# Local transformer on Trainium2: inverse key norms spread over the partitions by two transfers in place of a matmul

## The chip, the cores and the metric

The kernel runs on one core of one Trainium2 chip. The core has a matrix engine (PE, with its weight loads listed apart as PEld), a vector engine (DVE), a scalar engine (ACT), a general engine (POOL), and a queue (SP) from which this kernel issues all its DMA transfers. The engines run side by side and wait for one another by semaphores. The metric is the device time of one execution in microseconds (us), lower is better. It is given as the median of several runs. A separate execution was taken with the hardware profiler; every duration of single instructions comes from that one.

## The reference

The program is a chain of twelve stages on activations of 8 sequences of 256 tokens and 128 features, all in fp32: mixtures of experts, several kinds of attention, a state-space layer, and twice the same small local transformer of six layers. Only this local transformer is touched. Its attention, cut to what matters (`d` = 64, 16 heads, `w` = 32):

```python
def l2norm(t):
    return t / jnp.maximum(jnp.linalg.norm(t, axis=-1, keepdims=True), 1e-12)

def attn_layer(x, Wqkv, qs, ksc, Wo):
    q, k, v = jnp.split(x @ Wqkv, 3, -1)
    q, k, v = (sh(q), sh(k), sh(v))              # (batch, head, token, 64)
    q = l2norm(q) * qs
    k = l2norm(k) * ksc
    q = q * cos * scale + rotate_half(q) * sin * scale
    inv = 1.0 / scale
    k = k * cos * inv + rotate_half(k) * sin * inv
    out = local_attention(q, k, v)               # windows of 32 queries, 64 keys, softmax
    return out.transpose(0, 2, 1, 3).reshape(b, n, INNER) @ Wo
```

Each layer is `x = attn_layer(shift_tokens(x), ...) + x` and then `x = ffn_layer(shift_tokens(x), ...) + x`, where the second is a layer norm, a gated GELU network and a residual. What the change touches is the norm of the keys: every key of every head is divided by its length over the 64 features of the head.

## The kernel before, in words

**Groups and quads.** The 8 sequences are worked on in 4 groups of 2 sequences, so a tile has 128 partitions (features) and T = 512 columns (tokens). The 16 heads are taken four at a time: a *quad* is one group, one layer and four heads. Four heads of 64 features are 256 features, held as two tiles side by side (`j` = 0, 1), each with two heads over its 128 partitions. Six layers, four groups and four quads of each make 96 quads in a pass of the local transformer, 192 in the program.

**The pipeline.** `ffn2` runs three quads at a time, each in another phase. In one turn of its loop `q0` is projected and normalised, `q1` (the quad before) is scored, put through softmax and weighed with the values, and `q2` (the one before that) is turned back and handed on. The calls of a turn come in a fixed order: scores of `q1`, projection of `q0`, exponential of `q1`, `quad_back` of `q2`, `quad_norms` of `q0`, `quad_done` of `q2`, `quad_values` of `q0`, `quad_turn` of `q1`, `quad_scale` of `q0`, `quad_weigh` of `q1`. A wrapper (`_Ordered`) makes PE, DVE, ACT and POOL each keep the order in which their instructions are written, so a waiting instruction holds up everything behind it on its engine. Only the SP queue is ordered by the framework's scheduler.

**Pieces.** When the fourth quad of a group has been handed on, the group's output projection (`local_tail`: matmuls `wo_acc`, the residual `x`, the shifted copy `l_xs`, the layer norm `ln_c`, `ln_sq`, `ln_r`) is cut into pieces and put between the calls of one turn, and the gated network (`local_geglu`: matmuls `ge` and `w_acc`, GELU `l_gl`, product `l_ag`) into those of the next turn. So four turns make a cycle. If c is the number of the quad `q0` in its group, the turns c = 1 carry the tail, c = 2 the gated network, and c = 3 and c = 0 carry no pieces.

**The norms.** In `quad_project` PE makes `pp` (the projection), ACT squares it into `l_sq`, DVE multiplies it by the sine table (`l_y`) and by the cosine table (`l_yk` for the keys, `l_yq` for the queries), and four transfers exchange neighbouring partitions of the sine product into `l_yr` (the rotation's other half). In `quad_norms` the matrix `hsum` adds the squares over a head's partitions: four matmuls into one bank, and ACT makes the inverse square root, `l_rn`. Of each 32 rows of `l_rn` two hold something, one for each head; rows 0 to 63 belong to the queries and 64 to 127 to the keys. POOL adds the rotation's half to the keys (`l_yk`).

In `quad_scale`, 16 small matmuls with `hpick` bring the queries' inverse norms to where the softmax needs them (`tp`, which the profile calls bank, into `l_rq`), and two matmuls with `hrow` spread the keys' inverse norms from their two rows over each head's 64 partitions (`rb`). DVE then clamps `rb`, multiplies it into the keys and writes `l_kp`, and after that it adds the rotation's half to the queries (`l_yq`). `quad_scores` of the next turn reads both `l_kp` and `l_yq` in 128 small matmuls `sc`.

**Memory banks.** Most matmul results rotate through three double banks (`two`: `sc`, `pp`, `pp`, `ct`, `vp`, `et`, `rb`, `cx`, `cx`, and `ge`), so each of these waits until what was written three places before has been read. `l_sq` has two buffers.

Of the kernel before, what the change touches and what calls it, by code (L numbers as in the profile page):

```python
# [24 lines left out]
ALU = mybir.AluOpType  # L25
# [3 lines left out]
P = 128  # L29
B, S, D = 8, 256, 128  # L30
NB = 2
T = NB * S
# [6 lines left out]
WIN = 32  # L39
# [13 lines left out]
def _constants():  # L53

    f = np.float32
    p = np.arange(P)
    c = {}
    c["ident"] = np.eye(P, dtype=f)
    c["mean"] = np.full((P, P), 1.0 / P, f)
    c["ones"] = np.ones((P, P), f)  # L60
    c["iota"] = np.tile(np.arange(E, dtype=f), (P, 1))
    c["krow"] = (p % 32 == DH).astype(f)[:, None]
    c["eps"] = np.tile(
        np.array([1e-5, 2e-5, 2.0**-64, 0.5 * SH * math.log(2.0)], f), (P, 1)
    )
    blk = (p[:, None] // 64 == p[None, :] // 64).astype(f)
    c["blkm"] = blk / f(64)

    z = np.zeros((P, 32), f)
    z[:64, 0] = 1.0  # L70
    z[64:, 1] = 1.0
    c["hsum"] = z
    z = np.zeros((P, P), f)
    z[0::32, :64] = 1.0
    z[1::32, 64:] = 1.0
    c["hrow"] = z
    z = np.zeros((P, 4), f)
    for n, r in enumerate((0, 32, 1, 33)):
        z[r, n] = 1.0
    c["hpick"] = z  # L80

    r = np.zeros((P, P), f)
    for m in range(P):
        if m % 2 == 0:
            r[m + 1, m] = -1.0
        else:
            r[m - 1, m] = 1.0
    c["rot2"] = r

    sel = np.zeros((P, 4, P), f)  # L90
    for g in range(4):
        for j in range(4):
            for d in range(DH):
                sel[DH * (4 * g + j) + d, g, 32 * j + d] = 1.0
    c["sel"] = sel.reshape(P, -1)


    lev = [np.eye(P, dtype=f)]
    for i in range(7):
        n = 2**i  # L100
        q = p // n
        lev.append(((q[:, None] % 2 == 0) & (q[None, :] == q[:, None] + 1)).astype(f))
    c["lev"] = np.concatenate(lev, 1)

    c["cq"] = np.where(p[None, :] > p[:, None], f(NEG), f(0))
    c["ck"] = np.where(p[:, None] > p[None, :], f(NEG), f(0))
    one9 = np.zeros((P, 32), f)
    one9[:, DH] = 1.0
    c["one9"] = one9
    m = np.zeros((P, 2, 64), f)  # L110
    i, key = p % 32, np.arange(64)
    ok = (key[None, :] >= i[:, None]) & (key[None, :] <= i[:, None] + WIN)
    m[:, 0, :] = np.where(ok & ((p[:, None] >= 32) | (key[None, :] >= 32)), f(0), f(LNEG))
    m[:, 1, :] = np.where(ok, f(0), f(LNEG))
    c["lmask"] = m.reshape(P, -1)

    half = np.arange(0, 64, 2, dtype=f)
    inv_freq = f(1.0) / f(10000.0) ** (half / f(64))
    t = np.arange(S, dtype=f)
    fr = t[:, None] * inv_freq[None, :]  # L120
    fr = np.concatenate([fr, fr], -1).T
    base = (half + f(0.4 * 64)) / f(1.4 * 64)
    sc = base[None, :] ** ((t - f(S // 2)) / f(WIN // 2))[:, None]
    sc = np.concatenate([sc, sc], -1).T
    two = lambda a: np.concatenate([_partners(a.T).T] * 2, 0).astype(f)

    sgn = np.where(p[:64, None] < 32, f(1), f(-1))
    c["qcos"] = two(np.cos(fr) * sc * f(8.0))
    c["qsin"] = two(np.sin(fr) * sc * f(8.0) * sgn)
    c["kcos"] = two(np.cos(fr) * (f(1.0) / sc))  # L130
    c["ksin"] = two(np.sin(fr) * (f(1.0) / sc) * sgn)

    i = np.arange(DH // 2, dtype=f)
    th = np.power(f(10000.0), f(-2.0) * (i - f(1.0)) / f(DH))
    ang = t[:, None] * th[None, :]
    per = lambda a: np.tile(np.repeat(a.T, 2, axis=0), (NH, 1)).astype(f)
    c["rcos"] = per(np.cos(ang))
    c["rsin"] = per(np.sin(ang))

    groups = {  # L140
        "c1": ("ident", "mean", "ones", "iota", "krow", "eps"),
        "cs0": ("cq", "ck"),
        "cs1": ("lev", "blkm"),
        "cs2": ("hsum", "hrow", "hpick", "lmask", "qcos", "qsin", "kcos", "ksin"),
        "cs3": ("rot2", "sel", "ck", "one9", "rcos", "rsin"),
    }
    return {n: {k: c[k].astype(f) for k in ks} for n, ks in groups.items()}
# [10 lines left out]
def _partners(w):  # L158

    w = np.asarray(w)  # L160
    return w.reshape(w.shape[:-1] + (2, 32)).swapaxes(-1, -2).reshape(w.shape)
# [16 lines left out]
def _layout(inp):  # L178
# [72 lines left out]
    }  # L251
    a, at = {}, {}
    packs = {"pv": pv, "w0": w0, "wt": wt, "w1": w1, "w2": w2, "w3": w3, **_constants()}
    for name, parts in packs.items():
        a[name], at[name] = _pack(parts)
# [49 lines left out]
class _Net:  # L305
# [976 lines left out]
    def two(self, name):  # L1282
        return self.psp2.tile([P, 2, T], F32, tag="mm2", name=name)
# [48 lines left out]

    def quad_norms(self, q):

        nc = self.nc
        sp = self.ps()
        for s, (n, j) in enumerate((("q", 0), ("q", 1), ("k", 0), ("k", 1))):
            self.mm(sp[32 * s : 32 * s + 32, :], self.get("hsum"), q.sq[n][:, j, :])
        q.rn = self.work("l_rn", bufs=2)
        self.rsqrt(q.rn, sp, 2, scale=2.0**SH, shift=3)  # L1340
        nc.gpsimd.tensor_tensor(q.y["k"], q.y["k"], q.yr["k"], ALU.add)

    def quad_scale(self, q):


        nc = self.nc
        tp = self.ps()[:, :16].rearrange("p (m r) -> p m r", r=4)
        for b in range(NB):
            for x in range(2):
                for c in range(2):  # L1350
                    o = S * b + P * c + 64 * x
                    self.mm(tp[64 * c : 64 * c + 64, 2 * b + x, :], q.rn[:64, o : o + 64],
                            self.get("hpick")[:64, :])
        q.rq = self.work("l_rq", (P, 16), bufs=2)
        nc.vector.tensor_scalar(
            q.rq.rearrange("p (r m) -> p r m", m=4), tp.rearrange("p m r -> p r m"), 1e12, None,
            ALU.min)
        rb = self.two("rb")
        for j in range(2):
            r = slice(64 + 32 * j, 96 + 32 * j)  # L1360
            self.mm(rb[:, j, :], self.get("hrow")[r, :], q.rn[r, :])
        q.kp = self.kp[q.n % 2]
        nc.vector.scalar_tensor_tensor(
            q.kp[:, :, WIN:], rb.rearrange("p j (b s) -> p (j b) s", b=NB), 1e12,
            q.y["k"].rearrange("p j (b s) -> p (j b) s", b=NB), ALU.min, ALU.mult)
        nc.vector.tensor_tensor(q.y["q"], q.y["q"], q.yr["q"], ALU.add)

    def quad_scores(self, q):

# [363 lines left out]
```

## Time and profile before

| what | value |
|---|---|
| median of 3 runs | 5786.0 us (5776.98 to 5796.65) |
| the profiled execution's own time | 5776.49 us |
| its span (first to last instruction) | 5774.7 us |
| mean granted PE clock | 0.972 |
| PE busy | 5265.8 us, 91% |
| DVE / ACT / POOL busy | 59% / 42% / 17% |
| quads in the local transformer | 192, from about 960 to 5080 us of the span |
| four turns (one cycle), from the timeline | about 79 us |

A busy share is taken over all stages, and it says nothing on what a single stage waits for. The idle time of a group ("idle before") is the time for which its engine stood still just before its instructions, with the name of what ended the wait. "Issue" in the lists means that the engine waited for nothing that the profile shows. In the chain of waits the time is followed from the last instruction back to what released it.

### The profile page before, as it was taken

The numbers are of one execution on the slowest core, as the hardware profiler recorded it, in microseconds if no ns is written. First come the engines' busy times: TensorE is split into PE (matmuls) and PEld (weight loads), VectorE is DVE, ScalarE is ACT, GpSimd is POOL, SyncE is SP. The second block draws the span as 40 slices with busy tenths as digits, with TensorE's granted clock in tenths as the row PEclk, the third lists the DMA queues.
The fourth block names the chain that finished last, engine by engine and source line by source line (L and its number), as shares of the span: only waits on it lengthen the run. The fifth ranks groups of instructions, "written<-read, shape, count | busy, mean of one in ns | idle before, by whom it ended". The sixth has DMA issues, their size and how long they took to land.

```text
span 5774.7 us, 162548 instructions
## 1 busy us (share of the span) xinstructions
PE 5265.8 (91%) x74224; PEld 3046.1 (53%) x74224; DVE 3389.6 (59%) x4903; ACT 2446.6 (42%) x2948; POOL 985.8 (17%) x627
## 2 busy tenths in 40 slices
PE   9989997899999999999988899999998999989889
PEld 6756754555555555555544555555555555555446
DVE  4444455666666666666645666666666666645555
ACT  2233235444444444444434444444444444432442
POOL 0000022222222222222200222222222222200000
PEclk9999998999999999999989999999999999999899
DMA  1000001222222222222200222222222222210000
GB/s 64 1 1 1 1 1 43 76 89 85 90 86 84 94 78 93 81 95 80 76 22 11 84 85 88 81 92 79 94 79 90 88 86 83 76 44 1 1 1 8
DMA packets 116702, 347.82 MB, mean 60 GB/s; under 512 B 20401, under 2 KB 34610, under 8 KB 115762
## 3 DMA queue, kind: packets, MB, share of 16 engines
q1 hardware_dynamic: 116018, 337.43, 16.8%
q8 instruction: 585, 9.58, 0.7%
q14 instruction: 99, 0.81, 0.0%
HBM read 45.51 MB, written 1.05 MB: 8 GB/s over the span
## 4 chain that ended last, share of the span: by engine, by line
PE 76%; DVE 10%; issue 7%; ACT 6%; POOL 0%; DMA 0%; DVEq 0%; SPq 0%; POOLq 0%; ACTq 0%
PE pp L296 13%; PE mm L351 10%; PE bank L296 9%; PE e_o L351 6%; PE wo_acc L296 5%; PE sc L296 5%; PE vp L296 5%; PE ge L296 5%; PE rb L296 4%; PE et L296 3%; DVE l_yq L296 3%; ACT l_sq L296 3%; PE ms L296 2%; PE w_acc L296 2%; PE cx L296 2%
## 5 line engine op out<-in xcount | busy, mean ns | idle before, releaser
L296 ACT ACTIVATE l_sq<-pp 128x1024 f32<-128x1024 f32 x384 | 393.1, 1024 | 1278.8 <-PE pp L296 1278.8
L296 PE MATMUL pp<-l_xs,wqkv 128*128 128x512 f32 x1536 | 735.4, 622 | 14.9 <-issue 4.1
L296 POOL TENSOR_TENSOR l_e<-l_e,l_rq 128x1024 f32<-128x1024 f32 x192 | 365.4, 1903 | 2109.1 <-DVE l_e L296 2041.9
L296 POOL TENSOR_TENSOR l_yk<-l_yk,l_yr 128x1024 f32<-128x1024 f32 x192 | 452.3, 2356 | 556.8 <-DMA l_yr<-l_y 529.2
L351 PE MATMUL mm<-x,m 128*128 128x512 f32 x1024 | 478.0, 607 | 0.0
L296 PE MATMUL sc<-l_kp,l_yq 64*32 64x64 f32 x24576 | 321.3, 229 | 164.9 <-issue 134.7
L296 PEld LDWEIGHTS pp<-l_xs,wqkv 128*128 128x128 f32 x1536 | 286.1, 197 | 327.9 <-issue 302.2
L296 PEld LDWEIGHTS sc<-l_kp,l_yq 64*32 64x32 f32 x24576 | 268.4, 107 | 273.3 <-issue 201.0
L351 PEld LDWEIGHTS e_o<-m,e_h 128*128 128x128 f32 x3072 | 363.0, 192 | 60.2 <-issue 59.7
L296 PE MATMUL vp<-wqkv,l_xs 128*128 128x256 f32 x1536 | 382.8, 392 | 0.1
L296 PEld LDWEIGHTS vp<-wqkv,l_xs 128*128 128x128 f32 x1536 | 276.4, 190 | 190.3 <-issue 160.9
L351 PE MATMUL e_o<-m,e_h 128*128 128x128 f32 x3072 | 363.5, 275 | 0.0
L296 DVE TENSOR_REDUCE l_mx<-sc 128x16 f32<-128x1024 f32 x192 | 234.7, 1222 | 209.5 <-PE sc L296 209.4
L296 PE MATMUL wo_acc<-l_ct,wo 128*128 128x512 f32 x768 | 346.1, 594 | 0.0
L296 DVE SCALAR_TENSOR_TENSOR l_kp<-rb,l_yk 128x1024 f32<-128x1024 f32 x192 | 235.1, 1225 | 186.2 <-PE rb L296 182.5
L296 PEld LDWEIGHTS cx<-l_w,l_at 64*32 64x32 f32 x12288 | 255.4, 107 | 162.3 <-ACT l_at L296 70.5
L296 PE MATMUL cx<-l_v,l_at 64*32 64x65 f32 x12288 | 299.3, 229 | 11.3 <-issue 11.1
L296 PE MATMUL cx<-l_w,l_at 64*32 64x65 f32 x12288 | 294.7, 229 | 9.1 <-issue 6.9
L296 DVE TENSOR_TENSOR l_y<-pp,l_ksin 128x1024 f32<-128x1024 f32 x192 | 234.7, 1222 | 101.7 <-ACT l_sq L296 101.6
L351 PEld LDWEIGHTS mm<-x,m 128*128 128x128 f32 x1024 | 189.8, 195 | 197.0 <-issue 170.0
L296 PE MATMUL ge<-t,w 128*128 128x512 f32 (+1 forms) x576 | 282.1, 614 | 9.6 <-DVE l_yq L296 5.3
L296 DVE TENSOR_TENSOR l_cx<-cx,l_rc 128x512 f32<-128x512 f32 x384 | 265.5, 691 | 13.2
(277 smaller groups left out, 9223.8 us busy)
## 6 DMA issues: line engine op xcount, KB each, us to landing
l_yr<-l_y SPq DMA_DIRECT2D x768, 256.0 KB, 2.4
l_w<-l_v SPq DMA_DIRECT2D x192, 390.0 KB, 3.5
wqkv<-in_f_wqkv SPq DMA_DIRECT2D x48, 384.0 KB, 3.9
l_w<-l_v SPq DMA_DIRECT2D x192, 65.0 KB, 3.1
wo<-in_f_wo SPq DMA_DIRECT2D x12, 512.0 KB, 3.5
m<-in_m_w SPq DMA_DIRECT2D x16, 256.0 KB, 5.4
w<-in_f_w SPq DMA_DIRECT2D x12, 341.0 KB, 2.9
w<-in_f_w SPq DMA_DIRECT2D x12, 192.0 KB, 2.4
```

Of the source, the lines that this page charges most:

```text
L296: r = f(*args, **kw)
L351: self.nc.tensor.matmul(out, lhsT=lhsT, rhs=rhs, start=start, stop=stop)
```

## The change

The matmuls `rb` go, and with them the table `hrow`. So that transfers can take their place, `hsum` is filled in differently: instead of one column for each of the two heads it has sixteen equal columns for each. Every 32 rows of the sum then hold the first head's norm sixteen times and the second's sixteen times. Two transfers of the SP queue copy each of these rows four times, to 4 neighbouring partitions, which fills 128 partitions with 64 for each head (`q.rk`, a tile that takes its turn in the two buffers of `l_sq`). They are issued in `quad_norms`, after the inverse square root. The DVE instruction that makes `l_kp` reads `q.rk` in place of `rb`. The addition of the queries' halves (`l_yq`) is moved ahead of it. `hpick` takes the second head's row from 16 instead of 1.

```diff
     z = np.zeros((P, 32), f)
-    z[:64, 0] = 1.0
-    z[64:, 1] = 1.0
+    z[:64, :16] = 1.0
+    z[64:, 16:] = 1.0
     c["hsum"] = z
-    z = np.zeros((P, P), f)
-    z[0::32, :64] = 1.0
-    z[1::32, 64:] = 1.0
-    c["hrow"] = z
     z = np.zeros((P, 4), f)
-    for n, r in enumerate((0, 32, 1, 33)):
+    for n, r in enumerate((0, 32, 16, 48)):
         z[r, n] = 1.0
     c["hpick"] = z
...
     def quad_norms(self, q):
...
         q.rn = self.work("l_rn", bufs=2)
         self.rsqrt(q.rn, sp, 2, scale=2.0**SH, shift=3)
+        q.rk = self.work("l_sq", (P, 2, T), bufs=2)
+        for j in range(2):
+            nc.sync.dma_start(q.rk[:, j, :], q.rn[64 + 32 * j : 96 + 32 * j, :].unsqueeze(1)
+                              .to_broadcast([32, 4, T]))
         nc.gpsimd.tensor_tensor(q.y["k"], q.y["k"], q.yr["k"], ALU.add)
 
     def quad_scale(self, q):
...
-        rb = self.two("rb")
-        for j in range(2):
-            r = slice(64 + 32 * j, 96 + 32 * j)
-            self.mm(rb[:, j, :], self.get("hrow")[r, :], q.rn[r, :])
+        nc.vector.tensor_tensor(q.y["q"], q.y["q"], q.yr["q"], ALU.add)
         q.kp = self.kp[q.n % 2]
         nc.vector.scalar_tensor_tensor(
-            q.kp[:, :, WIN:], rb.rearrange("p j (b s) -> p (j b) s", b=NB), 1e12,
+            q.kp[:, :, WIN:], q.rk.rearrange("p j (b s) -> p (j b) s", b=NB), 1e12,
             q.y["k"].rearrange("p j (b s) -> p (j b) s", b=NB), ALU.min, ALU.mult)
-        nc.vector.tensor_tensor(q.y["q"], q.y["q"], q.yr["q"], ALU.add)
```

On PE, 192 turns lose two matmuls each (four instructions with their weight loads). DVE, ACT and POOL keep their instructions. The SP queue gets 384 transfers; in its order they stand between the four `l_yr` and the two `l_w` of the same quad.

More of the change, by code (lines that the diff above doesn't have):

```diff
@@ L143, in _constants @@
         "cs1": ("lev", "blkm"),
-        "cs2": ("hsum", "hrow", "hpick", "lmask", "qcos", "qsin", "kcos", "ksin"),
+        "cs2": ("hsum", "hpick", "lmask", "qcos", "qsin", "kcos", "ksin"),
         "cs3": ("rot2", "sel", "ck", "one9", "rcos", "rsin"),
```

## The prediction

> **What bounds the kernel now.** I read the page first: PE is busy almost throughout, and the instructions that go are on PE. Their own row, from the groups of PE between 1200 and 2800 us (80 turns), comes next, then the rows on the page for who waits for them and for the nearest transfers.
>
> ```profile
> PE 5265.8 (91%) x74224; PEld 3046.1 (53%) x74224; DVE 3389.6 (59%) x4903; ACT 2446.6 (42%) x2948; POOL 985.8 (17%) x627
> ...
> L296 DVE SCALAR_TENSOR_TENSOR l_kp<-rb,l_yk 128x1024 f32<-128x1024 f32 x192 | 235.1, 1225 | 186.2 <-PE rb L296 182.5
> ...
> q8 instruction: 585, 9.58, 0.7%
> ...
> l_yr<-l_y SPq DMA_DIRECT2D x768, 256.0 KB, 2.4
> l_w<-l_v SPq DMA_DIRECT2D x192, 390.0 KB, 3.5
> ```
>
> ```profile
> L296 PE MATMUL rb<-l_rn,sb_cs 32*128 32x512 f32 x320 | 90.2, 640 | 0.0
> ```
>
> So rb costs PE 90.2 / 80 = 1.13 us a turn busy, 1.06 from its first start to the next matmul's. At most 192 x 1.06 = 204 us can be won. What is really won depends on what PE meets next, so I went through one cycle of four turns by the chain of waits and the timeline. A plain turn, c = 0, in the chain of 2009 to 2027:
>
> ```profile
> 2018.96 0.56 PE bank L296 x16
> 2019.52 1.08 PE rb L296 x4
> 2020.60 0.03 issue
> 2020.63 0.02 DVEq L296
> 2020.65 0.05 issue
> 2020.70 0.09 DVE l_kp L296
> 2020.79 1.05 issue
> 2021.85 1.23 DVE l_yq L296
> 2023.07 0.04 issue
> 2023.12 0.45 PE sc L296 x28
> 2023.56 1.32 issue
> 2024.88 1.21 PE sc L296 x74
> ```
>
> The reader is to see two things. The chain runs rb, l_kp, l_yq, then sc, so the matmul and the DVE order are on the path here. And after 28 of the sc matmuls PE stands still for 1.32 us with nothing to wait for: "issue". I take that for the supply of instructions: 9.58 MB in 585 packets are 16 KB each, and cx and sc are together 256 matmuls with as many weight loads, within about 5 us. In the turn c = 1 the same sc ran without the gap, after a pause. Two rows of ACT and DVE, of c = 0 and c = 1:
>
> ```profile
> 2019.21 1.02 ACT L296 COPY l_at<-et 128x1024 f32<-128x1024 f32 x1
> ```
>
> ```profile
> 2045.58 0.68 DVE L296 TENSOR_TENSOR ln_c<-l_xs,bank 128x512 f32<-128x512 f32 x1
> ```
>
> ```profile
> 2046.97 1.13 PE L296 MATMUL bank<-ln_sq,sb_c 128*128 128x512 f32 x2 [1.31 <-ACT ln_sq L296]
> ```
>
> cx needs l_at, which ACT has ready only at 2020.23: rb lay over that wait. And the layer norm of c = 1 stands on DVE behind l_kp and l_yq, and PE waits 1.31 us for it.
>
> **What is removed, turn by turn.** *c = 0.* cx started at 2020.51, when rb was issued. Without rb PE is done with the small matmuls at 2019.45 and then waits for l_at, 2020.23 and some 0.06 us of signalling (the l_sq to hs hand-over takes 0.04 to 0.06): 2020.29. Gain 0.22, not 1.06. *c = 3.* l_at ends at 2082.87, so cx goes at 2082.93 in place of 2083.21: 0.28.
>
> What comes after cx in these two turns? The l_yq wait also goes: l_rq ends at 2019.74, l_yq follows to 2020.96, l_kp to 2022.19, against 2023.07 for the pair before. The sums could start at 2022.40 (cx 1.48 us, then the mask matmuls, 0.59) in place of 2023.12. But I hold that the gap behind it grows by as much: [...] So sc ends earlier by what cx starts earlier, and no more. I count 0.22 and 0.28.
>
> *c = 1.* Here PE gains little before cx, since the mean matmul between needs l_xs, ready at 2042.96, and ran at 2043.11. But DVE had l_rq at 2042.22 to 2042.37, then waited 0.93 us for rb. With no wait, l_yq and l_kp follow at once (1.14 us apart), and ln_c starts at 2044.67 in place of 2045.58: 0.91 earlier, so the variance matmul at 2046.06. cx is done by then. The instruction supply may bite as the pause shrinks; I take 0.75 of 0.91.
>
> *c = 2.* rb runs at 2063.94, and behind it ge, w_acc and cx follow without a gap until 2069.2. l_at has been ready since about 2062.4, and the GELU and l_ag of the third chunk move with ge. Full 1.06. The end of sc keeps its gap of 0.47 us, as cx moves too.
>
> Sum: 0.22 + 0.28 + 0.75 + 1.06 = 2.31 us a cycle, with 48 cycles 111 us.
>
> **What is added.** *Two transfers a turn.* No row shows this one. By size the nearest is l_yr, 256 KB in 2.4 us; between ends of 2.4 and 3.5 (l_w, also within the chip) I take 2.4. l_rn is ready at 2017.50, the SP queue has issued the four l_yr by 2017.75 (2014.42 plus 3.33), and an issue takes some 0.6 (l_w: 0.57 and 0.67). The second goes at 2018.4 and lands at 2020.8, at 3.5 us 2021.9. DVE asks for it at 2020.96. In the late case l_kp ends at 2023.15, 0.08 after l_yq did before, and sc has that much room within its gap. So zero; what hides it is vp, et, the small matmuls and l_yq. In c = 1 and c = 2 the pieces give 6 and 4 us more. On SP, l_w stands behind: it is ready to issue at 2019.34 and the two are out by about 2019.1, so nothing; its reader is the next turn's cx. The next l_yr comes 10 us later.
>
> *The DVE instruction reading SBUF in place of a bank.* The l_yq addition reads SBUF on both sides and takes 1217 ns, l_kp 1225. Bounds -0.1 and +0.1 us, value zero; only c = 1 has it on the path. *One bank fewer in the rotation*: sc then follows et, which l_at has emptied, in place of rb, which l_kp emptied; a slight gain, counted in the start of sc. *l_sq shared*: the turn's next user, the square of the queries, comes after sc, which needs l_kp anyway: zero. *hsum with equal columns* has the same shape: zero.
>
> [...] On the supply of instructions, the row is the 1.32 us of issue. [...] c = 0 and c = 3 would gain the whole wait, 0.72 and 0.77, and c = 1 0.91: 3.46 a cycle, 166 us. The row decides against it. [...]
>
> **The rivals.**
> *A, the gap moves with sc.* If [...] the gap mostly falls elsewhere, the 3.46 above hold: 5620. For it: some bursts may have no gap. Against: 134.7 us of issue waits before sc in the waits of PE. Chance 0.12.
> *B, the transfers crowd the instruction blocks.* 512 KB more a turn, ahead of l_w, on the DMA engines that also bring PE's blocks. [...] Against: between the last l_yr landing and l_w there is a hole of a microsecond, and DMA is at a quarter of its time. Chance 0.07.
> *C, slower: the transfers land late.* The place is l_kp on DVE in c = 0 and c = 3. Up to 2023.2, 4.8 us after the second issue, it is free; then each microsecond costs two a cycle, and with the 1.8 us of c = 1 and c = 2 against it the change turns slower at 5.7 us. At 7 us (the page's loads take up to 11) it is 2 x 2.2 - 1.8 = 2.6 a cycle, +125 us: 5911. For it: a source that repeats rows is not in the trace. Chance 0.10.
>
> [...]
>
> **How the numbers follow.** My forecast has 0.66, and weak gains (c = 0 and c = 3 lose half a microsecond) another 0.05, near 5750. Against the profiled execution's own time, 5776.5, 111 us give 5665; the median of the runs shown stands 9.5 higher, so I name 5786 - 111 = 5675. The forecast's own bounds are 1.2 us a cycle (nothing in c = 0 and c = 3, 0.3 and 0.9 in the others), 5728, and 3.4, 5623. The range, 5612 to 5770, holds these, most of A and the weak gains, with 10 us for the spread of the runs; B and C are left out. A measurement of this kernel can tell some 0.3% (17 us) from no change. Faster: 0.66 + 0.12 + 0.05 = 0.83; within 0.3%: 0.07; slower: 0.10.
>
> **What would show it.** Right: no rb; cx in plain turns starts some 0.06 us after l_at, with that wait named; the plain turns shrink by a quarter microsecond, the issue gap before or in sc grows; c = 2 shrinks by about 1.0, c = 1 by 0.7 to 0.9; l_kp starts at the end of l_yq. Wrong: l_kp waiting for DMA; an issue gap above 2 us in c = 0; plain turns shorter by 0.7 (A); turns of c = 2 shorter by less than 0.8.

## The result: 4% slower, and the profile after

The changed kernel takes 6014.52 us (median of 4 runs, 5986.69 to 6023.72), the kernel before 5781.51 in the same comparison: a ratio of 1.039, 95% interval 1.0358 to 1.0423. A gain of 111 us was forecast; the loss is 233. The profiled execution has a span of 6021.9 us (before 5774.7) and a mean granted PE clock of 0.926 (before 0.972).

The page after; of the last two lines the last number is the median from issue to landing:

```profile
PE 5250.6 (87%) x73456; PEld 3079.8 (51%) x73456; DVE 3426.0 (57%) x4903; ACT 2446.6 (41%) x2948; POOL 1069.9 (18%) x627
...
q1 hardware_dynamic: 171314, 438.05, 26.3%
q8 instruction: 579, 9.49, 0.6%
...
L292 DVE SCALAR_TENSOR_TENSOR l_kp<-l_sq,l_yk 128x1024 f32<-128x1024 f32 x192 | 256.6, 1336 | 312.4 <-DMA l_sq<-l_rn 312.4
...
l_sq<-l_rn SPq DMA_DIRECT2D x384, 256.0 KB, 4.2
l_w<-l_v SPq DMA_DIRECT2D x192, 390.0 KB, 6.3
```

The 192 matmul pairs are gone, yet PE is hardly less busy. In place of 182.5 us of waiting for rb, `l_kp` waits 312.4 us for the transfers. The two new transfers take 4.2 us in the median, not 2.4 (the first 3.9, the second 5.9), and `l_w` behind them takes 6.3 where it took 3.5. The waits of PE, before:

```profile
PE sc L296 <- issue: 134.7, 122, 2.9
...
PE cx L296 <- issue: 17.9, 34, 1.1
...
PE bank L296 <- POOL l_xs L296: 3.0, 2, 1.5
```

And after:

```profile
PE sc L292 <- DVE l_kp L292: 199.4, 67, 4.7
PE cx L292 <- issue: 104.8, 47, 4.6
PE bank L292 <- POOL l_xs L292: 90.4, 48, 1.9
PE cx L292 <- ACT l_at L292: 71.4, 91, 1.1
...
PE sc L292 <- issue: 46.7, 85, 2.7
```

Columns: us in total, times, longest. The wait of cx for `l_at` is there as forecast, 0.8 us each time. So are three that were not forecast: sc waits for `l_kp`, cx stands for "issue" (104.8 us, 17.9 before), and the matmul that forms the layer norm's mean (the profile calls it bank) waits for the shifted copy `l_xs` that POOL makes (90.4 us, 3.0 before). A *stand* is, from here on, a wait of PE that the profile puts down to issue; those before sc and cx are the ones that count here. One plain turn, c = 0, in the chain of waits (start, length, what):

```profile
2081.16 0.72 ACT l_rn L292
...
2082.90 5.88 DMA l_sq<-l_rn
2088.79 0.04 DVEq L292
2088.82 0.05 issue
2088.87 1.24 DVE l_kp L292
2090.11 0.04 issue
2090.15 1.91 PE sc L292 x108
2092.07 0.63 issue
2092.69 0.46 PE sc L292 x14
2093.15 2.00 PE pp L292 x2
```

The second transfer needs 5.88 us from its issue; everything up to sc hangs on it. The last line hides another cost: two pp matmuls take 2.00 us, and 1.06 in the kernel before (from 2026.08 there). PE had stood still for 2.90 us until 2088.95, and afterwards its matmuls run at about half the speed: the granted clock is 0.50 from 2090 to 2096, where it was 1.00 from 2023 to 2028 before.

By kind of turn, the median length from one pp to the next (turns between 1200 and 2800 us, read from the starts in the trace):

| kernel | c = 0 | c = 1 (tail) | c = 2 (gated network) | c = 3 | sum |
|---|---|---|---|---|---|
| before | 16.45 | 23.86 | 22.75 | 16.00 | 79.06 |
| after | 19.28 | 26.10 | 21.50 | 18.25 | 85.14 |
| after without transfers (e1) | 17.08 | 24.80 | 21.48 | 16.29 | 79.66 |
| e1 with a copy on DVE (e5) | 16.63 | 23.31 | 21.79 | 16.37 | 78.10 |
| before + dead transfers (e10) | 19.35 | 24.56 | 22.69 | 17.47 | 84.06 |
| before + dead transfers, late (e12) | 16.87 | 23.86 | 22.83 | 16.47 | 80.03 |

With means in place of medians the cycle grows by 5.27 us; 48 cycles make 253 us, against 247 between the two spans. So the loss lies in these turns: the plain ones and the tail lose, the gated network gains. The table covers part of the first pass, and differences of a few tenths in it do not carry over to the whole: e1 has a longer cycle here and a shorter run.

### The profile page after: what moved, and what is told of

The parts are those of the page before. It is cut to its first block, busy times and chain, and to the rows that moved or that the text cites. A ratio compares the mean times of both kernels' runs of the same rounds, so it can differ in the third digit from the quotient of the medians.

```text
span 6021.9 us, 162141 instructions
## 1 busy us (share of the span) xinstructions
PE 5250.6 (87%) x73456; PEld 3079.8 (51%) x73456; DVE 3426.0 (57%) x4903; ACT 2446.6 (41%) x2948; POOL 1069.9 (18%) x627
## 3 DMA queue, kind: packets, MB, share of 16 engines
q1 hardware_dynamic: 171314, 438.05, 26.3%
## 4 chain that ended last, share of the span: by engine, by line
PE 69%; ACT 9%; DVE 8%; DMA 6%; issue 5%; POOL 2%; SPq 0%; DVEq 0%; ACTq 0%; POOLq 0%
PE pp L292 14%; PE mm L347 9%; PE bank L292 8%; DMA l_sq<-l_rn 6%; PE sc L292 6%; PE e_o L347 6%; PE wo_acc L292 5%; PE ge L292 4%; PE cx L292 3%; ACT l_sq L292 3%; PE vp L292 3%; PE ms L292 2%; PE w_acc L292 2%; ACT lv L292 2%; DVE l_kp L292 2%
## 5 line engine op out<-in xcount | busy, mean ns | idle before, releaser
L292 PE MATMUL pp<-l_xs,wqkv 128*128 128x512 f32 x1536 | 818.1, 681 | 8.2 <-POOL l_v L292 3.5
L292 PE MATMUL sc<-l_kp,l_yq 64*32 64x64 f32 x24576 | 358.9, 258 | 246.8 <-DVE l_kp L292 199.4
L292 PEld LDWEIGHTS pp<-l_xs,wqkv 128*128 128x128 f32 x1536 | 319.8, 220 | 373.9 <-issue 356.8
L292 PEld LDWEIGHTS sc<-l_kp,l_yq 64*32 64x32 f32 x24576 | 301.0, 120 | 367.2 <-DVE l_kp L292 237.9
L292 DVE SCALAR_TENSOR_TENSOR l_kp<-l_sq,l_yk 128x1024 f32<-128x1024 f32 x192 | 256.6, 1336 | 312.4 <-DMA l_sq<-l_rn 312.4
L292 PE MATMUL cx<-l_w,l_at 64*32 64x65 f32 x12288 | 318.1, 245 | 125.7 <-ACT l_at L292 71.4
L292 PEld LDWEIGHTS cx<-l_w,l_at 64*32 64x32 f32 x12288 | 274.1, 114 | 227.0 <-issue 106.8
L292 PE MATMUL cx<-l_v,l_at 64*32 64x65 f32 x12288 | 323.3, 246 | 50.5 <-issue 50.5
L292 PEld LDWEIGHTS cx<-l_v,l_at 64*32 64x32 f32 x12288 | 270.3, 114 | 54.6 <-issue 54.6
```

The costliest lines, as they stand in the source:

```text
L292: r = f(*args, **kw)
```

## The experiments

**Transfers, or all the rest?** The changed kernel without its transfers (e1); the keys are multiplied by their squares, so it leaves the key norms out:

```diff
-        q.rk = self.work("l_sq", (P, 2, T), bufs=2)
-        for j in range(2):
-            nc.sync.dma_start(q.rk[:, j, :], q.rn[64 + 32 * j : 96 + 32 * j, :]...)
+        q.rk = q.sq["k"]
```

> The changed kernel without its two transfers: DVE multiplies the keys by their squares, which are in SBUF already, so the key norms are left out; order and engines are as changed. Theory L (the transfers land late, 4.2 us in the median, DVE and then PE stand for them in the plain turns, and PE's clock is halved after the stand): the plain turns fall to about 16.2 (c=0) and 15.7 us (c=3) and the first matmuls of the next turns to 3.70 us. Theory N (what is left: in c=1 the l_yq addition, moved ahead, runs beside POOL's l_xs copy, which takes 1.6 in place of 0.6 us, and the layer norm's mean waits): c=1 stays about 1 us longer than before, 24.9. Both together: -0.2 +1.0 -1.2 -0.3 = -0.7 us a cycle, about 5750 us. L alone, as the forecast had it: 5675. If neither is the cause (the order, or the freed PE time itself): above 5950.

Measured: 5768.83 us, ratio 0.9978 (0.9967 to 0.9988). The transfers cost 246 us, some 4%; without them the rest brings 13 us, not 111. Two things were wrong, then, and each needed its own runs. The kernel before with the order of the two DVE instructions alone (e2):

```diff
+        nc.vector.tensor_tensor(q.y["q"], q.y["q"], q.yr["q"], ALU.add)
         q.kp = self.kp[q.n % 2]
         nc.vector.scalar_tensor_tensor(...)
-        nc.vector.tensor_tensor(q.y["q"], q.y["q"], q.yr["q"], ALU.add)
```

> The kernel before with one thing changed: the l_yq addition ahead of l_kp; rb is still a matmul. Theory N: the l_xs copy of c=1 takes 1.6 us here too and the mean waits for it, about +0.9 before cx, but ln_c comes sooner, so c=1 ends up some 0.4 us shorter; the plain turns do not change since the supply of instructions ends their sc: about 5765. Rival (the DVE chain rb, l_kp, l_yq held the plain turns, and the gap moves with sc): 0.7 less in each plain turn too, about 5700. If the order alone is what hurts: above 5800.

Measured: 5787.88 us, 1.0016 (1.0006 to 1.0026). Both sc inputs are ready 0.9 us earlier in a plain turn (12.1 in place of 13.01 us after its pp). PE is done with what stands ahead of sc only shortly before the old time, so sc itself starts 0.06 (c = 0) and 0.36 us (c = 3) earlier, and the turn stays as long (16.29 and 16.04): the stand before sc grows from 134.7 to 158.4 us. What sc wins at its start it loses in the stand, which speaks against rival A. The turns c = 1 lose 0.9 us. Why is seen in the groups of POOL; the number after the comma is the mean in ns. Before:

```profile
L296 POOL COPY l_xs<-x 64x512 f32<-64x512 f32 x96 | 57.8, 602 | 330.2 <-DVE x L296 330.1
```

With the order alone:

```profile
L296 POOL COPY l_xs<-x 64x512 f32<-64x512 f32 x96 | 135.8, 1414 | 329.9 <-DVE x L296 329.8
```

The same copy takes more than twice as long when the `l_yq` addition, which has both operands in SBUF and none in a bank, runs beside it; in the changed kernel the mean is 1444. In the turns c = 1 the trace has the copy ending 0.55 us after `l_yq` does. That speaks against the reordering, and the forecast did not look there. Two runs take the copy off POOL:

```diff
-        self.nc.gpsimd.tensor_copy(xs[:64], x[:64])
+        self.nc.vector.tensor_copy(xs[:64], x[:64])
```

once on top of the kernel without transfers (e5),

> The kernel without transfers (the key norms left out) and with the lower half of the l_xs copy on DVE in place of POOL. Theory N (DVE's two SBUF operations and POOL's copy slow each other, and PE's mean matmul and then its clock pay for it): the copy is done before l_yq starts, PE's 88 us of waits for POOL l_xs go, c=1 falls from 24.8 to about 22.9 us, the whole to about 5680, which is what the forecast had for transfers that cost nothing. Rival (c=1 is long for another reason, such as the instruction supply in cx): less than 30 us gained, above 5740.

and once on the kernel before with the new order, which keeps rb (e6):

> The kernel before with rb still a matmul, the l_yq addition ahead of l_kp, and the lower half of the l_xs copy on DVE. Theory N: the +0.9 us that the order cost in c=1 goes, and ln_c comes 0.9 us sooner than before: c=1 about 23.0 in place of 23.86, plain turns as before: 5735 to 5745. Rival (the order is worth nothing): 5775 to 5785.

Measured: 5721.05 us, 0.9893 (0.9873 to 0.9913), and 5763.68 us, 0.9968 (0.9954 to 0.9982). On DVE the copy takes 414 ns, and the turns c = 1 of e5 fall to 23.31, that is 0.55 below before in the median (0.22 in the mean). The second of these computes everything and beats both kernels, the one before by 0.3%. But in e5 the plain turns, 16.63 and 16.37, are still no shorter than with rb, and its 60 us fall far short of the 166 that rival A had for transfers that cost nothing. The waits of PE in e5:

```profile
PE sc L292 <- issue: 157.0, 120, 3.2
...
PE cx L292 <- issue: 39.6, 45, 1.4
```

Together 196.6 us of stands, against 152.6 before (134.7 and 17.9): 44 us more, 42 of them in the plain turns, or 0.44 in each of these 96. What is left of rb's time there after the wait for `l_at`, the stands take back.

**How the loss goes with the traffic.** Two other ways to bring as many bytes to the same place: 128 different rows, each read once (e3; what arrives is not the spread norms),

```diff
-            nc.sync.dma_start(q.rk[:, j, :], q.rn[64 + 32 * j : 96 + 32 * j, :].unsqueeze(1)
-                              .to_broadcast([32, 4, T]))
+            nc.sync.dma_start(q.rk[:, j, :], q.rn)
```

> The changed kernel with each transfer reading all 128 partitions of l_rn once, in place of 32 of them four times; bytes, packets of 2 KB, waits and order are the same, and what arrives are not the spread norms. Theory R (repeated reads from 32 partitions are slow): landing falls from 4.2 to between 2.4 and 3, l_kp follows l_yq in the plain turns, time as without transfers, 5750 to 5780. Theory V (the volume, 512 KB more a turn, is slow by itself): landing stays near 4 and the time above 5950.

and rows read four times, but taken from both halves of the partitions, with `hpick` and its small matmuls fitted to the new places (e4):

```diff
-        for s, (n, j) in enumerate((("q", 0), ("q", 1), ("k", 0), ("k", 1))):
+        for s, (n, j) in enumerate((("q", 0), ("k", 0), ("q", 1), ("k", 1))):
...
-            nc.sync.dma_start(q.rk[:, j, :], q.rn[64 + 32 * j : 96 + 32 * j, :].unsqueeze(1)
+            nc.sync.dma_start(q.rk[:, j, :], q.rn[32 + 64 * j : 64 + 64 * j, :].unsqueeze(1)
```

> The changed kernel with the key rows of l_rn at partitions 32 to 63 and 96 to 127 in place of 64 to 127 (the sums in the order q0, k0, q1, k1, and the queries' small matmuls reading 128 rows). Everything is still computed. Theory R [...] landing falls to about 3 us, the plain turns lose some 1.3 us each against the changed kernel, about 5880. If it is the repeat of a row itself, or the volume, that is slow: unchanged, 6015.

Measured: 5826.67 us, 1.0080 (1.0054 to 1.0107), and 5918.51 us, 1.0244 (1.0210 to 1.0279). The bytes are equal; the time of the DMA engines is not. From the share of q1 (16.8% before, 21.3, 24.0 and 26.3% in e3, e4 and after), times the spans, less before's, over 192 turns, the transfers occupy all 16 engines for 1.4, 2.3 and 3.2 us a turn. The mean 2 KB packet in the trace (1200 to 2800 us) goes from 89 to 149 and 209 ns. Against the kernel without transfers the loss is 58, 150 and 246 us. So it rises with the time for which the engines are held, though not in proportion. In the waits it is the data that shows: from e1 to e3, e4 and after, PE waits 11.6, 49.1, 122.8 and 199.4 us for `l_kp` before sc, while its stands before sc and cx, 194.5, 177.2, 155.6 and 151.5 us, do not grow. Whether what else the engines carry would hold PE up without that wait, these runs do not tell.

**The wait, or the traffic?** First the other side of the changed kernel: its copy on DVE (e7, the same two lines as above).

> The changed kernel with the lower half of the l_xs copy on DVE. Theory N on top of theory L: c=1 loses its 1.9 us wait for POOL, some 90 us in all: 5925. If the loss of c=1 comes from the late transfers and the halved clock alone: unchanged, 6000 to 6015.

Measured: 6001.43 us, 1.0379 (1.0356 to 1.0402). The turns c = 1 shrink by 1.9 us (1.5 from e1 to e5), and the plain turns grow by 0.6 and 0.5. Of the 90 us expected 13 came. Then the kernel before with the transfers added, and nobody reading them (e10):

```diff
         self.rsqrt(q.rn, sp, 2, scale=2.0**SH, shift=3)
+        q.rk = self.work("l_sq", (P, 2, T), bufs=2)
+        for j in range(2):
+            nc.sync.dma_start(q.rk[:, j, :], q.rn[64 + 32 * j : 96 + 32 * j, :].unsqueeze(1)
+                              .to_broadcast([32, 4, T]))
```

> The kernel before, rb and order as they were, with the two transfers issued in addition and read by nobody. Theory L (they cost by being waited for): the time of before, within 15 us. Theory V (their traffic itself holds up l_w, the SP queue or the blocks of PE's instructions): 30 to 120 us slower.

Measured: 6007.78 us, 1.0398 (1.0369 to 1.0426): the whole loss, about twice what was expected at most, with rb, the old order and no wait for the data. Its PE waits,

```profile
PE sc L296 <- issue: 230.9, 125, 4.1
...
PE cx L296 <- issue: 47.0, 40, 4.6
```

and a plain turn of it in the chain:

```profile
2073.64 1.23 DVE l_yq L296
2074.87 0.04 issue
2074.91 0.45 PE sc L296 x29
2075.36 3.51 issue
2078.87 1.70 PE sc L296 x96
2080.57 2.86 PE pp L296 x3
```

This is a plain turn like the one that the prediction showed, with 3.51 us in place of 1.32 at the same point of sc, and the inputs of sc there. The stands are 125 us longer than before in the run, and the pp matmuls after them 86 us, out of 229 in the span. The pp group, before and here:

```profile
L296 PE MATMUL pp<-l_xs,wqkv 128*128 128x512 f32 x1536 | 735.4, 622 | 14.9 <-issue 4.1
```

```profile
L296 PE MATMUL pp<-l_xs,wqkv 128*128 128x512 f32 x1536 | 821.5, 683 | 9.5 <-POOL l_w L296 3.7 <-issue 3.3 <-POOL l_xs L296 1.0
```

That the stands are waits for instruction blocks can be read from the packets of the queue q8, which the page lists as instruction, 16 KB each. Their number goes with PE's instructions: 585 for 148448 matmuls and weight loads before, 579 for 146912 after, so 6 packets fewer for 1536 instructions, 256 to a packet. Before the change 97 stands in cx and sc of plain turns are longer than half a microsecond, and 97% of them end between 1.2 and 1.6 us after such a packet has ended; in e10 it is 95% of 98. Of random moments between 9 and 16 us of these turns under a tenth lie so. In the turns c = 3 the two kernels reach the stand at the same time, 13.8 us into the turn. The packet that ends it starts at 12.66 before and at 13.94 in e10, and takes 1.0 and 1.1 us; the stand lasts 1.1 and 2.7 us (medians). PE has got just as far by then, and the block comes later. In c = 2 the same transfers cost nothing (22.69 against 22.75); there cx starts some seven microseconds later, after they have landed. The loss of c = 1 (0.7 us) is slow pp: with cx after the landing there too, its stands do not grow, but its `l_rn` ends 0.7 us later.

**Is it the clock?** Half-speed pp after the stands (granted clock 0.50 in the turn above) might itself be the cause of the loss. Dead matmuls fill the stand in the turns c = 0 and c = 3, in double banks (e8),

```diff
             self.piece(pieces)
+            if q0 and q0.n % 4 in (0, 3):
+                for m in range(2):
+                    fill = self.two("fill")
+                    for j in range(2 - m):
+                        self.mm(fill[:, j, :], self.get("ident"), q0.sq["q"][:, j, :])
```

> The changed kernel with three dead matmuls (identity by the queries' squares, 2.6 us) at the end of each plain turn, where PE stands for l_kp; nothing reads them. Theory C ([...] the next turn's first matmuls run at half speed): PE is kept busy, the pp matmuls of the turns after are back at 3.70 us in place of 4.7 to 4.9, and the kernel gets faster by 1.0 to 1.2 us in each of 96 turns although it does more: about 5905. If the halved clock does not come from the stand: 6015 or slower.

and, in case the double banks of the rotation held sc up, in a single one (e9):

```diff
+                fill = self.ps()
+                for _ in range(3):
+                    self.mm(fill, self.get("ident"), q0.sq["q"][:, 0, :])
```

> As the filled kernel, but the three dead matmuls go to the single bank that is free at that place, so that they take no turn in the three double banks (in the filled kernel the second tile and the mask had to wait for l_cx, behind l_kp on DVE). Theory C: pp and sc run at full speed, l_kp still ends at about 15.8 us of a plain turn and sc follows in 1.5: c=3 17.3, c=0 17.3, c=1 about 24.9, 4.2 us a cycle less than the changed kernel, about 5815. If the halved clock costs little, and the late transfers by themselves make the loss: above 5950.

Measured: 6028.06 us, 1.0424 (1.0403 to 1.0444), and 6023.22 us, 1.0422 (1.0400 to 1.0444). The groups of e9 begin with pp at full speed again (681 ns after, 616 here), and its mean granted clock is 0.949:

```profile
L292 PE MATMUL pp<-l_xs,wqkv 128*128 128x512 f32 x1536 | 726.6, 616 | 10.2 <-DVE l_mx L292 4.1 <-DMA wqkv<-in_f_wqkv 3.6 <-POOL l_xs L292 1.0
```

Nothing is won in sum, so the half clock alone is not the cause. It is not free either: by the means of the turns, e9 wins 1.0 us in c = 1 (25.61 to 24.60) and 0.5 in c = 0 (19.52 to 19.03), and loses 1.2 in c = 3 (18.28 to 19.45), which pays for the dead matmuls and had no slow pp to lose. How much filling costs and how much the full clock gives, no run separates. With pp on time everything in the turn c = 0 starts about a microsecond earlier, and `l_kp` still starts only at 14.7 us (15.6 after), because the second transfer lands 6.0 us after its issue. In the changed kernel the wait for the data lies beside the stands; e10 has taken the wait away and the stands fill its place.

**Place, or volume?** The kernel before once more, with two dead transfers of the same form and size, but issued after `l_cx`, 13.9 us into a plain turn (e12):

```diff
+            if not j:
+                rk = self.work("l_y2", (P, 2, T), bufs=2)
+            nc.sync.dma_start(rk[:, j, :], cx[64 + 32 * j : 96 + 32 * j]
+                              .rearrange("p x n d -> p (x n d)").unsqueeze(1)
+                              .to_broadcast([32, 4, T]))
```

> The kernel before, with two more transfers of the same form and size as the changed kernel's (32 partitions read four times into 128, 256 KB each), but issued late: their source is the row half of l_cx, so they start after l_cx, about 14 us into the turn, and nobody reads what they write. Theory that their time of day is what costs (they hold the DMA engines [...]): most of the loss is gone, 5786 to 5830 us. Rival, that the volume costs whenever it moves (each turn's instruction supply shares the engines somewhere): 5980 to 6020, as with the same transfers early (6007.8).

Measured: 5795.53 us, 1.0026 (1.0016 to 1.0035). Of 230 us some 15 are left. Page, waits and a plain turn of the chain:

```profile
q1 hardware_dynamic: 171314, 438.12, 25.7%
q8 instruction: 585, 9.58, 0.7%
...
l_y<-l_cx SPq DMA_DIRECT2D x384, 256.0 KB, 4.0
l_w<-l_v SPq DMA_DIRECT2D x192, 390.0 KB, 3.5
```

```profile
PE sc L296 <- issue: 136.2, 124, 2.3
...
PE cx L296 <- issue: 23.7, 39, 1.1
```

```profile
2016.08 1.14 PE sc L296 x70
2017.21 1.32 issue
2018.53 0.54 PE sc L296 x35
```

The same number of packets and bytes, landing in 4.0 us, and the stand is 1.32 us again. They hold the engines for 2.7 us a turn by the share of q1 (3.2 when early), more than the 2.3 of e4, which cost 150 us against its base. Their place in the turn decides: between 9 and 15 us come the blocks that PE stands for in cx and sc.

**Is `l_w` part of the queue?** The two `l_w` transfers, which stand behind the new ones, moved after `l_kp`: first in e6, which has no other transfers there (e13),

```diff
-        nc.sync.dma_start(w[32:], v[:96])
-        nc.sync.dma_start(w[:32, 1::2], v[96:, 0::2])
...
+        w, v = q.v
+        nc.vector.memset(v[:, :, :, 64:], 1.0)
+        nc.sync.dma_start(w[32:], v[:96])
+        nc.sync.dma_start(w[:32, 1::2], v[96:, 0::2])
```

> The kernel before with the queries' sum first and the l_xs copy on DVE (5763.7), and the two l_w transfers (195 KB each) issued after l_kp in place of ahead of the scores' norms. If l_w's own traffic is part of the stand before sc: the stands of plain turns shrink by up to half, some 0.6 us in 96 turns, 5700 to 5735. Rival, the stand is the latency of one block alone: 5760 to 5770. If l_w then comes too late for cx or crowds the next turn's blocks: above 5780.

and then in e4 with the copy on DVE (e14):

> Everything computed, the norms spread by transfers of both halves (each 16 rows of 64 partitions' source, 151 ns packets; 5918.5 alone), the l_xs copy on DVE, and l_w issued after l_kp. If the queue of transfers in front of PE's instruction blocks is what costs, taking l_w's part out of it returns some: 5830 to 5870. Rival, the spreading transfers alone crowd the blocks: 5885 to 5900, the copy's gain only.

Measured: 5775.88 us, 0.9987 (0.9976 to 0.9998), and 5847.73 us, 1.0115 (1.0100 to 1.0130). In e13 nothing is won (e6 has 0.9968). Its waits show the stands only moved about; the memset that the edit adds on DVE, 72 ns, costs sc no more waiting (12.2 us, where e6 waits 14.4 for `l_kp`):

```profile
PE sc L296 <- issue: 161.3, 137, 3.6
...
PE pp L296 <- issue: 17.3, 11, 3.1
```

So `l_w` alone is not what the blocks wait for before the change. In e14 two things changed against e4, and e4 with the copy alone was not run. The copy gave 0.5% from e2 to e6, 0.9% from e1 to e5, but 0.1% from the changed kernel to e7. From 1.0244 that would leave 1.016 to 1.023; the measured 1.0115 puts 0.4 to 1.2% down to `l_w`. Behind long transfers it seems to be a part of the crowd. A last run has e4 with the copy on DVE and two dead matmuls in the stand (e11):

```diff
-        self.nc.gpsimd.tensor_copy(xs[:64], x[:64])
+        self.nc.vector.tensor_copy(xs[:64], x[:64])
...
+            if q0 and q0.n % 4 in (0, 3):
+                fill = self.ps()
+                for _ in range(2):
+                    self.mm(fill, self.get("ident"), q0.sq["q"][:, 0, :])
```

> Everything is computed, with transfers: the key rows in both halves, the lower half of the l_xs copy on DVE, two dead matmuls (1.7 us) in the single bank at the end of each plain turn. If landing, POOL and clock are the three causes, their remedies add up: l_kp ends at 14.4 in plain turns, sc at full speed, c=3 and c=0 about 16.0 to 16.5, c=1 23.3, c=2 21.6: 77.5 us a cycle, about 5690. If the supply of instructions ends the plain turns, they stay at 16.5 to 17: 5720 to 5760. If traffic costs by itself: above 5800.

Measured: 5868.33 us, 1.0152 (1.0131 to 1.0173), 0.9% below e4. That can be the copy's gain and no more, or in part the full clock's (pp is at 611 ns); no run separates the two. No version that spreads the norms by transfers is faster than the kernel before; the best, e14, is 1.2% slower.

## Why the prediction was wrong, step by step

- **c = 2, 1.06 us: right.** The turn shrank by 1.25 (after) and 1.27 (e1).
- **c = 1, 0.75 us: wrong in sign.** The step "with no wait, l_yq and l_kp follow at once" was right, and it put `l_yq` beside POOL's copy of `l_xs`. The forecast took `l_xs` as ready at the old time; the copy grew from 602 to 1444 ns and the mean matmul waited 1.9 us. Without transfers the turn lost 0.94. With the copy on DVE it gained 0.55 in the median, 0.22 in the mean.
- **Plain turns, 0.22 and 0.28 us: wrong.** cx did go 0.22 and 0.28 us sooner (10.23 and 10.17 us into the turn in e5, 10.45 before). That the `l_yq` wait is worth nothing held (e2). That "sc ends earlier by what cx starts earlier" did not: even with neither transfers nor the POOL clash (e5) the turns grew by 0.18 and 0.37 (over both passes 0.17 and 0.25), and the stands in cx and sc with them. Why they grow, no run shows.
- **The two transfers at zero: the step that failed most.** Mis-sized twice. The landing was taken as `l_yr`'s 2.4 us, with 3.5 as the far end; the second transfer took 5.9. And the cover named for them, vp, et, the small matmuls and `l_yq`, can hide a wait for data but not the use of the engines, which the sum put at nothing: dead, with nobody waiting, the same transfers cost 4.0% (e10). They hold the engines for 3.2 us a turn.
- **`l_w` behind them, nothing:** as a wait, yes (PE's loads waited for it 5.3 us in all the run). As traffic it seems to count, 0.4 to 1.2% in e14.
- **The DVE instruction from SBUF, ±0.1 us:** held. The mean of 1336 ns is the clash with POOL's copy again; with the copy on DVE it is 1235.
- **The stand, which grows by what cx gains.** It was right not to count the earlier start of sc as won: in e2 the stand before sc grows from 134.7 to 158.4 us. The forecast let the stand grow only by what cx gained, though, where the runs show that it also grows with what else is on the DMA engines: 152.6 us before sc and cx in the kernel before, 277.9 with dead transfers.
- **A source that repeats rows,** named under rival C, was sized like `l_yr`. The new transfers are slow by their packets: the mean 2 KB packet takes 209 ns, 149 in e4 and 89 in e3, with the same number of bytes.
- **The rivals.** A is refuted by e2 and e5 together. C named the right wait: a landing 5.9 us after the second issue is just past its turning point of 5.7, and its own sum would have been 0.4 us a cycle, 19 us. B named what e10 shows, transfers that crowd PE's blocks (in c = 3 the packet that ends the stand starts at 13.94 us in place of 12.66), but for a time within 0.3% of before, where the plain turns of e10 lose 2.9 and 1.5 us. It had a chance of 0.07 because of a hole of a microsecond and engines busy a quarter of the time. That share is a mean; what counts is the 5 us around cx. The two mechanisms run side by side. B's alone is enough for the whole loss (e10); that C's alone would be, no run shows.

Still open: whether the blocks that come 1.3 us late in e10 are held up within the DMA engines or earlier on their way; and how much of the 86 us of slow pp in e10 could be had back, as the dead matmuls that restored the clock took time and instructions themselves.

## What to carry to other kernels

A transfer that nobody waits for is not free: here two of 256 KB a turn, read by nobody, cost 4.0% when they were issued ahead of cx (e10) and 0.3% when they were issued after `l_cx` (e12). Where PE goes through hundreds of small matmuls, its instruction blocks are DMA traffic too (585 packets of 16 KB here), and "issue" gaps in PE's waits can mark the stretch to keep free of other traffic. Cost a transfer by the time for which it holds the engines, by its packets and not its bytes (the same 512 KB held them for 1.4, 2.3 and 3.2 us a turn in e3, e4 and after), and test it cheaply by adding it dead to the kernel before, at two places. When a DVE instruction moves, look at what POOL does at its new place: the copy of `l_xs` went from 602 to 1414 ns.

## What was not expected of the hardware

- A 2 KB packet within the chip took 89 ns from 128 different partitions, 149 ns when the two transfers read rows four times from different halves of the partitions, and 209 ns when both read four times from the same half (means between 1200 and 2800 us). Such reads after `l_cx` (e12) took 169 ns, at another time of the turn.
- An instruction block's packet took about 1.0 us, and PE went on 1.2 to 1.6 us after its end. With two 256 KB transfers under way it started 1.3 us later (12.66 and 13.94 us into the turns c = 3).
- A POOL copy of 64x512 fp32 went from 602 to 1414 ns beside a DVE addition with both operands in SBUF.
- After PE has stood still for two microseconds or more, its next matmuls often run at half speed: pp averaged 681 ns after and 622 before, at mean granted clocks of 0.926 and 0.972. In e10 the first two pp of a turn took over 800 ns in 1 of 52 turns whose longest wait of PE in the 6 us before was under 1 us, in 9 of 59 at 1 to 2 us, in 32 of 51 at 2 to 3, and in 24 of 28 above. Filling the waits brought pp back to 616 ns, and the time stayed.
